# Splitting the convolution taps of two images between TensorE and VectorE, and when the gates of the second image stand in the queues

## The chip, the cores and the metric

The kernel runs on one core of a Trainium2 chip. The metric is the device time of one execution in microseconds (us). The kernel before took 3125.04 us, the median of three runs (3124.64 to 3130.11).

A core has five engines that run at the same time, each with its own queue of instructions in fixed order: TensorE (PE in the profile) multiplies matrices, VectorE (DVE) does elementwise work and reductions, ScalarE (ACT) functions such as Gelu, GpSimd (POOL) elementwise work and indirect DMAs, and SyncE (SP) issues plain DMAs. An instruction that waits holds back everything behind it in its queue.

## The reference

Two layers work on four images of 384 channels and 32×32 pixels. The first is an attention layer followed by a small MLP. The second, where the change is, adds a sum of depthwise convolutions and then a mixture of four experts:

```python
x = x + _L1_conv_ref(_ln_c(x), w77, b77, w53, ...)   # depthwise 7x7 + 5x3 + 3x5 + two separable ones
t = _to_tokens(x)
t = t + _L1_ffn_ref(_ln_t(t), gate_w, gate_b, w1, b1, w2, b2)

# in _L1_ffn_ref
probs = softmax(x @ gate_w + gate_b)                 # 4 experts, the two best of each token are kept
h = gelu(x @ w1[e] + b1[e])                          # 384 -> 1536
y = h @ w2[e] + b2[e]                                # 1536 -> 384
out = sum over e of masked[e] * y[e]
```

Everything is float32. All five convolutions fold into one 7×7 kernel per channel: 49 taps.

## The kernel before

The program has three parts. The first two, the projections and the attention (until about 1506 us of the span), are left as they are. The third, `rest_phase`, goes through the images b = 0 to 3.

**Per image.** `front(b)` loads the attention's output and x, projects (`project`: nine matmuls L977 for each half image, sums on VectorE L980), and runs the first layer's MLP (`net`: L999, L1012, Gelu L1022, L1016, L1029, the sum on VectorE L1030) for both halves. `banks` (L990) says how many accumulators the MLP's first matmuls rotate through: six for images 0 and 2, three for the others. `normalise` makes the normalised halves, and `image` (L1068) writes them into the single padded tile `img`, which holds one image at a time: the next image can be written only when the taps of the last have been read.

**Taps.** An image has 3 chunks of 128 channels by 32 rows, so 96 rows of a chunk. `convolve` (L1089) runs the taps on VectorE as one multiply-add each, all rows of a chunk at once (1024 elements per partition). Of image 0, `taps_by_matmul` gives 56 of the 96 rows to TensorE instead: chunk 2 whole in two parts of 16 rows (512 columns), and rows 8 to 32 of chunk 1 in two parts of 12 (384 columns). A part is 49 taps × 2 halves of matmuls with 64×64 diagonals of the tap's weights (L1133), two copies, two matmuls that fold the sums (L1144), and one addition on VectorE (L1147). The diagonals are made by GpSimd (L1115) and lie in the second pair of expert weight buffers, `wts[1]`, which is loaded by `preload` when image 0's taps are done.

**Gates and dispatch.** `gates(b)` multiplies the image by the gate weights (`gate_ps` L661, `logits_ps` L673), transposes it into token rows (`row_ps` L87, statistics on VectorE L89, a copy L92), picks two experts per token on VectorE and normalises the rows (L1191). `scatter(b)` ranks the tokens (`before_ps` L755, `count_ps` L757), and sends 16 indirect DMAs on GpSimd's queue (L1199) that write the rows into their experts' slots in DRAM; behind the first of them it works out which expert each block of the group has. `dispatch` is the two together.

**Blocks.** The experts run over blocks of 128 tokens of one expert, in four groups of 13, 16, 16 and 22; group b can begin when image b has been scattered. A block is 12 steps (`e_ps` L1294, Gelu L1297, `y_ps` L1272); its tokens come by an indirect DMA (L1243, transposed at L1256) that waits for the scatters of its group, its weights in two halves by indirect DMAs (L1262) into two pairs of buffers in turn, fetched three halves ahead; its end is the addition L1275.

**Order.** Image 0 is done ahead of the blocks (`first`), with image 1's front between its taps. Then image 0's dispatch is written, with the front of image 2 between its steps. The rest hangs on the blocks: `others` is a generator of side work (the taps of images 1, 2, 3, their dispatches, the front of image 3), and after each step of a block `more` adds 0.05 and 1.36 us to two clocks, of VectorE's and TensorE's work, and takes side steps, each with its two costs, while VectorE's clock is behind TensorE's:

```python
clock[0] += 0.05
clock[1] += 1.36
...
while clock[0] < clock[1] and spend(todo):
    pass
```

In `others`, the dispatch of image b is spent between the taps of image b + 1: step 2 and later of the taps takes the front of the next image (`side` or `later` by turns). A scheduler orders what is written; `pin` (`keep_in_program_order`) fixes an instruction's place on its engine, and `marks[b]` with `issue_after` holds the first additions of image b's taps behind a given instruction.

Of the kernel before, what the change touches and what calls it, by code (L numbers as in the profile page):

```python
# [13 lines left out]
ALU = mybir.AluOpType  # L14
# [8 lines left out]
KC = C // P  # L23
# [47 lines left out]
def bcast(ap, dim, n):  # L71

    dims = [list(d) for d in ap.ap]
    dims[dim] = [0, n]
    return bass.AP(ap.tensor, ap.offset, dims)
# [818 lines left out]
def rest_phase(tc, cst, x, ao_d, ins, xs_d, y_d, x2_d, out):  # L894
# [9 lines left out]
    with ExitStack() as es:  # L904
# [82 lines left out]

        def net(b, xs, rstd):

            banks = [(ps_h, "h", None)] * 3 + ([(ps_y, "y", 2)] * 2 + [(ps_y, "t", None)] if b in (0, 2) else [])  # L990
            if True:
                scale = to_partitions(nc, (small, ps_m, "m"), ident, one, rstd)
                scale_sb = work.tile([P, TOK], F32, tag="scale", name="scale")
                nc.scalar.copy(scale_sb, scale)


                ps = ps_m.tile([P, TOK], F32, tag="m", name="u_ps")
                for k in range(KC):
                    nc.tensor.matmul(ps, fold[:, k, :], xs[:, k, :], start=(k == 0), stop=(k == KC - 1))  # L999
                u = small.tile([P, TOK], F32, tag="u", name="u")  # L1000
                nc.vector.tensor_tensor(u, ps, scale_sb, ALU.mult)
                yield 1.4, 3.5

                po = ps_m.tile([P, TOK], F32, tag="m", name="o32_ps")
                pend = []
                for f0 in range(0, NF + 3, 3):
                    phs = []
                    for f in range(f0, min(f0 + 3, NF)):
                        pool, tag, bufs = banks[f % len(banks)]
                        ph = pool.tile([P, TOK], F32, tag=tag, name="f_ps", **({"bufs": bufs} if bufs else {}))  # L1010
                        lo = f % 4 * 32
                        nc.tensor.matmul(ph, c1t[lo : lo + 32, f // 4, :], u[lo : lo + 32, :], start=True, stop=True)  # L1012
                        phs.append((f, ph))
                    for f, hs in pend:
                        lo = f % 4 * 32
                        nc.tensor.matmul(  # L1016
                            po[lo : lo + 32, :], cp1t[:, f, :], hs, start=(f < 4), stop=(f >= NF - 4)
                        )
                    pend = []
                    for f, ph in phs:  # L1020
                        hs = hid.tile([P, TOK], F32, tag="hs", name="hs", bufs=HS)
                        nc.scalar.activation(hs, ph, AF.Gelu)  # L1022
                        pend.append((f, hs))
                    yield 0.0, 2.2
                o32 = small.tile([P, TOK], F32, tag="u", name="o32")
                nc.scalar.copy(o32, po)
                for m in range(KC):
                    ps = ps_h.tile([P, TOK], F32, tag="h", name="ffn_ps")
                    nc.tensor.matmul(ps, spread[:, m * P : (m + 1) * P], o32, start=True, stop=True)  # L1029
                    nc.vector.scalar_tensor_tensor(  # L1030
                        xs[:, m, :], ps, cp2[:, m : m + 1], xs[:, m, :], ALU.mult, ALU.add
                    )
                yield 2.1, 2.7
# [45 lines left out]
        def convolve(b, xb, parts):  # L1079


            with tc.issue_after(marks[b]) if b in marks else nullcontext():
                for k in range(KC):
                    nc.vector.tensor_scalar_add(xb[:, k, :], xb[:, k, :], cbias[:, k : k + 1])
            acc = xb.rearrange("p k (y x) -> p k y x", x=IMG)
            for dy in range(7):
                for dx in range(7):
                    for k, y0, y1 in parts:
                        nc.vector.scalar_tensor_tensor(  # L1089
                            acc[:, k, y0:y1], img[:, k, dy + y0 : dy + y1, dx : dx + IMG],  # L1090
                            w7[:, k, dy, dx : dx + 1], acc[:, k, y0:y1], ALU.mult, ALU.add,
                        )

                    if b:
                        tc.keep_in_program_order(nc.vector.memset(pause, 0.0))  # L1095
                    yield sum(0.12 + 0.0337 * (y1 - y0) for _, y0, y1 in parts) + 0.06, 0.0
            if b + 1 < B:
                nc.sync.dma_start(x2_d[:, b * N : (b + 1) * N].rearrange("(k p) n -> p k n", p=P), xb)
# [1 line left out]

        wts = [[wp.tile([P, WROW], F32, name=f"w{i}{fh}") for fh in range(2)] for i in range(2)]

        def preload(w, keep=lambda ins_: ins_):
            for fh in range(2):
                keep(nc.sync.dma_start(w[fh], ins["w12"][fh * P : (fh + 1) * P, :]))

        none = wp.tile([P, 2, 1], F32, name="none")
        nc.vector.memset(none, 0.0)
        def taps_by_matmul(xb, parts):

            def diagonals(k, w):
                d = w[:, : 49 * 64].rearrange("p (t m) -> p t m", m=64)
                nc.gpsimd.tensor_tensor(  # L1115
                    d, bcast(half.unsqueeze(1), 1, 49),
                    bcast(w7[:, k].rearrange("p y x -> p (y x)").unsqueeze(2), 2, 64), ALU.mult,
                )
                return d

            half = small.tile([P, 64], F32, tag="half", name="half", bufs=1)
            nc.vector.tensor_tensor(half, ident[:, :64], ident[:, 64:], ALU.add)
            diag = {k: diagonals(k, w) for k, w in zip(dict.fromkeys(k for k, *_ in parts), wts[1])}
            yield
            for k, y0, ny in parts:
                n = ny * IMG
                sums = [ps_y.tile([P, TOK], F32, tag="y", name="tap_ps", bufs=2) for _ in range(2)]
# [52 lines left out]
        def gates(b):  # L1180

            xb, im = xbs[b], images[b]
            rows = [new_row() for _ in range(nj)]
            logits = ps_m.tile([P, TOK], F32, tag="m", name="logits_ps")
            yield from gate_logits(nc, (ps_m, hid), ident, gw, xb, logits)
            mean, rstd = yield from token_stats(nc, stp, ident, xb, cst["eps5"], rows, 2)
            shift = small.tile([P, nj, 1], F32, tag="g_shift", name="g_shift")
            nc.vector.scalar_tensor_tensor(shift, mean, -1.0, rstd, ALU.mult, ALU.mult)
            yield from gate_weights(nc, small, logits, gb, rstd, im["mask"], im["top"])
            for j, row in enumerate(rows):  # L1190
                nc.scalar.activation(row, row, AF.Identity, bias=shift[:, j, :], scale=rstd[:, j, :])  # L1191
                im["rows"].append(row)
            yield 0.0, 0.0

        def new_row():
# [21 lines left out]
        def scatter(b, pause):  # L1217
# [3 lines left out]
            for j, rows in enumerate(im["rows"]):  # L1221
                for s in range(2):
                    write(rows, im["pos"][:, j, s : s + 1])
                if j == 0:
# [3 lines left out]
                    else:  # L1228
                        part = number_of_blocks(counts[b], False)
                        parts = [(done, part, b % 2 == 1)]  # L1230
                        parts.append((part, number_of_blocks(counts[b + 1], False), b % 2 == 0))
                        block_list(nc, small, pc, g, parts, None)
                    yield 4.0, 0.0
                yield pause, 0.0
            g["after"] = list(scattered)
# [146 lines left out]
        def first(halves, later):  # L1382


            half, own = IMG // 2, 8
            rest = (IMG - own) // 2
            taps = taps_by_matmul(
                xbs[0], [(2, 0, half), (2, half, half), (1, own, rest), (1, own + rest, rest)]
            )
            next(taps)  # L1390
            yield from image(halves)
            for i, _ in enumerate(convolve(0, xbs[0], [(0, 0, IMG), (1, 0, own)])):
                for _ in range(2 + (i % 4 == 3)):
                    next(taps, None)
                if i % 7 < 5:
                    next(later, None)
# [2 lines left out]
                        for _ in steps:  # L1399
                            pass  # L1400
                yield
            preload(wts[1])

        def others():

            later = iter(())
            for b in range(1, B):  # L1410
                if b > 1:
                    yield from image(halves[b])
                side, later = later, ahead(b + 1, halves[b + 1]) if b > 1 else iter(())
                for t, cost in enumerate(convolve(b, xbs[b], [(k, 0, IMG) for k in range(KC)])):
                    for start, steps in ((2, side), (12, later)):
                        more = next(steps, None) if t >= start else None
                        if more:
# [2 lines left out]
                yield from side  # L1420
                yield from later
                later = dispatch(b, 0.0 if b + 1 < B else 2.6)
            yield 6.0, 0.0
            yield from later

# [18 lines left out]
            pass  # L1444
        center(nc, ps_m, "m", one, gw)
        todo = others()
        for _ in first(halves[0], ahead(1, halves[1])):
            pass
        after_it = ahead(2, halves[2])
        for i, _ in enumerate(dispatch(0)):  # L1450
            if i == 0:
                result(image(halves[1]))
            if i == 10:
                marks[1] = latest(mybir.EngineType.DVE)
            for _ in range(3 if i > 5 else 0):
                next(after_it, None)
        result(after_it)
        clock = [0.0, 0.0]

        def spend(steps):  # L1460
            cost = next(steps, None)
# [125 lines left out]
```

## Time and profile before

The profile is of one execution on the chip, which took 3141.26 us itself, 16 us above the median of the three runs.

| | before |
|---|---|
| median of 3 runs | 3125.04 us (3124.64 to 3130.11) |
| the profiled execution | 3141.26 us |
| its span, first to last instruction | 3139.3 us |
| PE busy | 2942.2 us (94%) |
| DVE busy | 1935.2 us (62%) |
| ACT busy | 1370.1 us (44%) |
| POOL busy | 1168.1 us (37%) |
| granted TensorE clock, mean | 0.971 |

"Busy" is the time in which an engine executes something. In the view by slices, each digit is the busy share of one of 40 equal slices in tenths, and PEclk the clock that TensorE was granted. In a timeline line, the numbers are the start, the duration, the engine, the line of the program, the operation, what it writes and reads, the shapes and how many records, and in brackets the idle time before it and what ended it. One float32 matmul leaves two records. In the chain of waits, each line is a piece of work that ended last: start, duration, engine, what, line.

### The profile page before, as it was taken

How to read it: one execution, taken by the hardware profiler on the slowest of the kernel's cores; microseconds unless marked ns; L12 is line 12 of the kernel's file. 1: busy time of each engine (PE TensorE's matmuls, PEld its weight loads, DVE VectorE, ACT ScalarE, POOL GpSimd, SP SyncE). 2: the span in 40 equal slices, each digit the busy share in tenths (PEclk: the TensorE clock that was granted, in tenths of full speed). 3: DMA queues.
4: the chain of work that ended last, by engine and by line, in shares of the span. 5: the costliest groups of instructions: out<-in, count | busy, mean ns of one | idle time of the engine just before them, and what ended most of it. 6: DMA issues, size and time to landing. Idle time of an engine off the chain costs nothing.

```text
span 3139.3 us, 63791 instructions
## 1 busy us (share of the span) xinstructions
PE 2942.2 (94%) x25591; PEld 2026.2 (65%) x25591; DVE 1935.2 (62%) x3576; ACT 1370.1 (44%) x2833; POOL 1168.1 (37%) x1132
## 2 busy tenths in 40 slices
PE   8997999999999999999889999958999899999996
PEld 4544776777777777777433447734678677777775
DVE  2226777878787877787485699998999400001101
ACT  1115667666666666666202233323343423333332
POOL 2224747474746464646200222222143221124412
PEclk9998999999999999999989989988999999999998
DMA  3796566656565646563400305610444144375842
GB/s 128 261 316 204 130 197 136 202 134 202 133 204 130 209 125 209 125 210 97 162 19 33 136 23 222 257 56 26 169 177 172 41 174 182 138 277 210 301 178 73
DMA packets 262792, 500.56 MB, mean 159 GB/s; under 512 B 134736, under 2 KB 186832, under 8 KB 254816
## 3 DMA queue, kind: packets, MB, share of 16 engines
q1 hardware_dynamic: 169168, 247.12, 25.6%
q0 software_dynamic: 43424, 227.84, 19.7%
q10 hardware_dynamic: 49904, 21.53, 3.5%
q8 instruction: 201, 3.29, 0.4%
q14 instruction: 95, 0.78, 0.1%
HBM read 543.58 MB, written 152.37 MB: 222 GB/s over the span
## 4 chain that ended last, share of the span: by engine, by line
PE 73%; issue 9%; DVE 7%; POOL 4%; DMA 4%; ACT 2%; another core or an unknown queue 0%; SPq 0%; POOLq 0%; ACTq 0%; DVEq 0%
PE e_ps L1294 16%; PE y_ps L1272 15%; PE t_ps L410 7%; PE sc_ps L227 7%; PE av_ps L227 6%; PE tabq_ps L227 5%; DVE xb L1089 3%; PE a_ps L420 3%; PE tap_ps L1133 2%; DMA s<-sd 2%; PE tv_ps L227 2%; POOL bias L353 1%; PE proj_ps L977 1%; PE row_ps L87 1%; PE tabk_ps L227 1%
## 5 line engine op out<-in xcount | busy, mean ns | idle before, releaser
L1294 PEld LDWEIGHTS e_ps<-xT,w 128*128 128x128 f32 x4824 | 654.5, 192 | 214.1 <-issue 10.7
L353 POOL TENSOR_TENSOR bias<-b,s 128x416 f32<-128x416 f32 (+24 forms) x656 | 659.3, 1043 | 179.0 <-DMA s<-sd 165.1
L1294 PE MATMUL e_ps<-xT,w 128*128 128x128 f32 x4824 | 669.4, 276 | 8.6 <-DVE pause L1095 2.4
L1272 PE MATMUL y_ps<-w,eh 128*128 128x384 f32 x1608 | 651.9, 489 | 13.9 <-ACT eh L1297 11.9
L1089 DVE SCALAR_TENSOR_TENSOR xb<-img,pack,xb 128x1024 f32<-128x1024 f32 (+1 forms) x539 | 616.8, 1203 | 0.0
L1297 ACT ACTIVATE eh<-e_ps,w 128x128 f32<-128x128 f32 x804 | 293.2, 367 | 719.3 <-PE e_ps L1294 658.9
L1262 POOL DMA_INDIRECT w<-in_w,row x134 | 169.4, 1264 | 727.1 <-PE y_ps L1272 302.8
L402 DVE TENSOR_REDUCE extra<-arow 128x32 f32<-128x32 f32 (+24 forms) x768 | 381.3, 555 | 9.7 <-ACT arow L391 5.6
L381 DVE CUSTOM_DVE_ANT_0 arow<-sc_ps,bias 128x1024 f32<-128x1024 f32 x256 | 312.6, 1221 | 101.8 <-POOL bias L353 57.3
L410 PEld LDWEIGHTS t_ps<-ident,arow 128*128 128x128 f32 x2048 | 221.1, 142 | 175.2 <-ACT aT L411 100.6
L391 ACT ACTIVATE arow<-arow,nm 128x1024 f32<-128x1024 f32 x256 | 302.5, 1182 | 66.6 <-DVE nm L381 66.6
L1275 DVE TENSOR_TENSOR yo<-y_ps,w 128x384 f32<-128x384 f32 x67 | 37.1, 553 | 460.3 <-PE y_ps L1272 460.3
L411 ACT COPY aT<-t_ps 128x512 f32<-128x512 f32 x512 | 278.6, 603 | 95.2 <-PE t_ps L410 94.9
L410 PE MATMUL t_ps<-ident,arow 128*128 128x128 f32 x2048 | 283.1, 282 | 16.5 <-ACT arow L391 16.5
L227 PE MATMUL sc_ps<-kk,qs 48*32 48x512 f32 x4096 | 278.3, 606 | 8.7 <-DVE nm L381 8.1
L1272 PEld LDWEIGHTS y_ps<-w,eh 128*128 128x128 f32 x1608 | 246.7, 192 | 23.6 <-ACT eh L1297 13.8
L227 PEld LDWEIGHTS av_ps<-aT,vb 128*64 128x64 f32 x4096 | 222.3, 137 | 51.3 <-ACT aT L411 41.2
L227 PE MATMUL av_ps<-aT,vb 128*64 128x128 f32 x4096 | 237.7, 274 | 0.0
L318 DVE STREAM_TRANSPOSE b<-tabk_ps 128x480 f32<-128x480 f32 x256 | 218.4, 981 | 23.6 <-PE tabk_ps L227 22.2
L227 PE MATMUL tabk_ps<-tab,kq 48*128 48x480 f32 x512 | 223.2, 583 | 5.7 <-DVE b L318 5.7
L227 PE MATMUL tabq_ps<-tab,kq 48*128 48x480 f32 x512 | 220.3, 579 | 2.1 <-ACT aT L411 1.4
L1199 POOL DMA_INDIRECT xs_d<-rows,pos x64 | 78.5, 1227 | 337.7 <-DVE xb L980 253.0
(211 smaller groups left out, 3253.9 us busy)
## 6 DMA issues: line engine op xcount, KB each, us to landing
sd<-st SPq DMA_DIRECT2D x128, 480.0 KB
s<-sd SPq DMA_DIRECT2D x256, 240.0 KB
xs_d<-zero POOLq DMA_DIRECT2D x8, 3072.0 KB
tvw<-in_tv SPq DMA_DIRECT2D x120, 192.0 KB
y_d<-yo SPq DMA_DIRECT2D x67, 192.0 KB
qk_d<-qk_sb POOLq DMA_DIRECT2D x48, 256.0 KB
qs<-qk_d SPq DMA_DIRECT2D x256, 48.0 KB
kq<-qk_d ACTq DMA_DIRECT2D x56, 192.0 KB
```

Source lines behind the costliest of these rows:

```text
L227: ins = nc.tensor.matmul(*args, **kw)
L318: turn = nc.vector.transpose(b2.rearrange("p e y x -> p x (e y)")[:, i + j], ps[:, j, : SPAN * IMG])
L353: nc.gpsimd.tensor_tensor(bias[:, y0:y1, :], bass.AP(b2.tensor, b2.offset + (e * IMG + y0) * IMG, [list(b2.ap[0]), [(step * IMG + 1) * IMG ...
L381: nc.vector.tensor_tensor_reduce(s["flat"], ps.rearrange("p h n -> p (h n)"), s["bias"].rearrange("p y x -> p (y x)"), -SCALE, BIG, ALU.ad ...
L391: nc.scalar.activation(s["flat"], s["flat"], AF.Exp, bias=s["nm"], scale=-1.0, accum_out=dn[:, y % YT : y % YT + 1])
L402: pin(nc.vector.tensor_reduce(ex[:, i, :], a[:, p0:p1, :].rearrange("p y x -> p x y"), AX.X, ALU.add))
L410: pin(nc.tensor.transpose(pt[:, j, :], s["flat"][:, k0 : k0 + P], ident))
L411: pin(nc.scalar.copy(aT[:, 4 * g : 4 * g + 4, s["y"] % YB, :], pt))
L1089: nc.vector.scalar_tensor_tensor(acc[:, k, y0:y1], img[:, k, dy + y0 : dy + y1, dx : dx + IMG], w7[:, k, dy, dx : dx + 1], acc[:, k, y0:y1 ...
L1272: nc.tensor.matmul(py, hs, w[:, o : o + C], start=(ff == 0), stop=(ff == NF - 1))
L1294: nc.tensor.matmul(ph, w[:, o : o + P], xT[k][:, c, :], start=(c == 0), stop=(c == KC - 1))
L1297: nc.scalar.activation(hs, ph, AF.Gelu, bias=w[:, o : o + 1])
```

## The change

It has five parts.

1. Of image 0, TensorE does 40 of the 96 rows (chunk 2 whole, and rows 24 to 32 of chunk 1 in one part of 256 columns), VectorE chunk 0 and 24 rows of chunk 1. VectorE's taps of image 0 are pinned in program order, and the rhythm in which TensorE's taps are written between them changes.
2. The diagonals are made once, ahead of image 0's taps, and used again: TensorE does rows 0 to 16 of chunk 2 of image 1, written between the steps of image 0's dispatch, and VectorE the other 80 rows. The two buffers that hold the diagonals are loaded at two times: `wts[1][1]` after image 0's taps, `wts[1][0]` after those of image 1.
3. The dispatch of image 1 is started at once after the taps of image 1; after its first step, image 2 is written into `img`, and the dispatch is spent whole before image 2's taps. From image 2 on the order is as before. The mark that holds an image's first additions behind is set in `scatter`, behind the block list, for every image.
4. TensorE's clock starts at 25 instead of 0, so side work is taken earlier. In `gates`, steps are added after every second row for images 1 to 3.
5. The MLP of image 2 rotates through three accumulators instead of six.

```diff
-            banks = [(ps_h, "h", None)] * 3 + ([(ps_y, "y", 2)] * 2 + [(ps_y, "t", None)] if b in (0, 2) else [])
+            banks = [(ps_h, "h", None)] * 3 + ([(ps_y, "y", 2)] * 2 + [(ps_y, "t", None)] if b == 0 else [])
...
-                        nc.vector.scalar_tensor_tensor(
+                        ins_ = nc.vector.scalar_tensor_tensor(
                             acc[:, k, y0:y1], img[:, k, dy + y0 : dy + y1, dx : dx + IMG],
                             w7[:, k, dy, dx : dx + 1], acc[:, k, y0:y1], ALU.mult, ALU.add,
                         )
+                        if not b:
+                            pin(ins_)
...
-        def preload(w, keep=lambda ins_: ins_):
-            for fh in range(2):
+        def preload(w, keep=lambda ins_: ins_, which=range(2)):
+            for fh in which:
...
-        def taps_by_matmul(xb, parts):
-            def diagonals(k, w):
-                d = w[:, : 49 * 64].rearrange("p (t m) -> p t m", m=64)
+        def diagonals(chunks):
+            half = small.tile([P, 64], F32, tag="half", name="half", bufs=1)
+            nc.vector.tensor_tensor(half, ident[:, :64], ident[:, 64:], ALU.add)
+            diag = {}
+            for k, w in zip(chunks, wts[1]):
+                diag[k] = w[:, : 49 * 64].rearrange("p (t m) -> p t m", m=64)
                 nc.gpsimd.tensor_tensor(
-                    d, bcast(half.unsqueeze(1), 1, 49),
+                    diag[k], bcast(half.unsqueeze(1), 1, 49),
...
+        def taps_by_matmul(xb, made, parts):
+            half, diag = made
...
                 im["rows"].append(row)
+                if b and j % 2:
+                    yield 0.0, 0.0
...
                         block_list(nc, small, pc, g, parts, None)
+                    marks[b + 1] = latest(mybir.EngineType.DVE)
...
-            half, own = IMG // 2, 8
-            rest = (IMG - own) // 2
-            taps = taps_by_matmul(
-                xbs[0], [(2, 0, half), (2, half, half), (1, own, rest), (1, own + rest, rest)]
-            )
-            next(taps)
+            half, own = IMG // 2, 24
+            taps = taps_by_matmul(xbs[0], made, [(2, 0, half), (2, half, half), (1, own, IMG - own)])
             yield from image(halves)
             for i, _ in enumerate(convolve(0, xbs[0], [(0, 0, IMG), (1, 0, own)])):
-                for _ in range(2 + (i % 4 == 3)):
+                for _ in range(1 + i % 4 // 2 + (i % 7 == 0)):
                     next(taps, None)
...
-            preload(wts[1])
+            preload(wts[1], which=(1,))
...
-            later = iter(())
+            half, later = IMG // 2, iter(())
             for b in range(1, B):
-                if b > 1:
+                if b > 2:
                     yield from image(halves[b])
                 side, later = later, ahead(b + 1, halves[b + 1]) if b > 1 else iter(())
-                for t, cost in enumerate(convolve(b, xbs[b], [(k, 0, IMG) for k in range(KC)])):
+                parts = [(k, 0, IMG) for k in range(KC - 1)] + [(KC - 1, half if b == 1 else 0, IMG)]
+                for t, cost in enumerate(convolve(b, xbs[b], parts)):
...
                 later = dispatch(b, 0.0 if b + 1 < B else 2.6)
+                if b == 1:
+                    yield next(later)
+                    yield from image(halves[2])
+                    yield from later
...
         todo = others()
+        made = diagonals((2, 1))
         for _ in first(halves[0], ahead(1, halves[1])):
             pass
-        after_it = ahead(2, halves[2])
+        taps, later = taps_by_matmul(xbs[1], made, [(2, 0, IMG // 2)]), ahead(2, halves[2])
         for i, _ in enumerate(dispatch(0)):
             if i == 0:
                 result(image(halves[1]))
-            if i == 10:
-                marks[1] = latest(mybir.EngineType.DVE)
-            for _ in range(3 if i > 5 else 0):
-                next(after_it, None)
-        result(after_it)
-        clock = [0.0, 0.0]
+            for steps in (taps, taps, taps, later, later, later) if i > 5 else ():
+                next(steps, None)
+        for steps in (taps, later):
+            result(steps)
+        preload(wts[1], which=(0,))
+        clock = [0.0, 25.0]
```

## The prediction

> **What bounds the kernel now.** I read the page's 40 slices first, each 78.5 us long.
>
> ```profile
> PE   8997999999999999999889999958999899999996
> DVE  2226777878787877787485699998999400001101
> PEclk9998999999999999999989989988999999999998
> ```
>
> TensorE (PE) is full from slice 21 on, but for one hole (5 and 8, from about 2041 us), where VectorE (DVE) stays at 9. The change touches only this part. So I cut it by the events of its code into windows: start and end, us, busy time by engine, granted TensorE clock, DMA share, GB/s.
>
> ```profile
> 1592.80:1764.50 171.70, 152.05 (x972) 56.48 (x964) 110.36 (x162) 24.13 (x44) 0.00 (x0) 0.91 0.07 26
> 1764.50:1796.30 31.80, 26.83 (x95) 13.74 (x95) 24.23 (x123) 13.05 (x23) 8.96 (x9) 0.89 0.76 270
> 1796.30:1849.30 53.00, 46.03 (x174) 16.46 (x173) 50.60 (x75) 20.36 (x35) 21.35 (x17) 0.84 0.15 50
> 1849.30:2068.00 218.70, 217.87 (x1326) 170.27 (x1325) 217.61 (x263) 69.70 (x180) 41.30 (x30) 1.00 0.45 174
> 2068.00:2128.60 60.60, 16.73 (x46) 8.15 (x44) 56.41 (x150) 10.52 (x16) 24.12 (x20) 0.67 0.24 85
> 2128.60:2200.00 71.40, 67.71 (x330) 36.37 (x331) 63.13 (x79) 28.82 (x57) 11.37 (x9) 0.95 0.05 15
> ```
>
> Row 1 is image 0's taps, bound by TensorE (152 of 172). Row 2 is image 0's gates up to image 1's first tap, row 3 ends at the first expert matmul. Row 4, the 13 blocks of group 0, has TensorE and VectorE both full. Row 5 is the hole: TensorE works 16.7 of 60.6 us. The timeline and the chain of waits say for what (time, duration, engine):
>
> ```profile
> 2046.02 2.77 PE L661 MATMUL gate_ps<-xb,pack 128*32 128x512 f32 x12
> 2128.61 0.90 PE L1256 MATMUL xT_ps<-ident,xg 128*128 128x128 f32 x3 [28.71 <-DMA xg<-xs_d,slot]
> 2131.53 4.92 PE L977 MATMUL proj_ps<-at,pack 128*128 128x512 f32 x6
> ```
> ```profile
> 2069.69 2.37 DVE xb L1089 x2
> 2073.43 4.30 ACT rows L1191 x7
> 2089.56 1.19 DVE xb L1089
> 2097.92 1.09 POOL xs_d L1199
> 2116.70 2.02 POOL xs_d L1199
> 2125.47 3.10 DMA xg<-xs_d,slot
> ```
>
> Gates of image 1 start in group 0's last block, at 2046. Their small VectorE steps stand between image 2's taps of 1.19 us, 16 scatters follow, and group 1's tokens arrive 82.6 us after the gate matmul.
>
> The groups of window 1 (busy us, mean ns of one, idle before) price the taps:
>
> ```profile
> L1089 DVE SCALAR_TENSOR_TENSOR xb<-img,pack,xb 128x1024 f32<-128x1024 f32 x49 | 62.6, 1278 | 0.0
> L1133 PE MATMUL tap_ps<-img,w 64*64 64x512 f32 x348 | 48.5, 624 | 0.0
> L1133 PE MATMUL tap_ps<-img,w 64*64 64x384 f32 x392 | 39.0, 495 | 0.0
> L1089 DVE SCALAR_TENSOR_TENSOR xb<-img,pack,xb 128x256 f32<-128x256 f32 x49 | 23.4, 477 | 0.0
> ```
>
> **What the Trainium skill says.** "TensorE: Matmul & The Clock Gate", section "What's actually happening": the array drops to half clock after an idle window and needs some 3.4 us of work to return. The trace agrees: after 28.7 us idle six projection records take 4.92 us (2.84 at 1603.9, with the clock up) and the clock reads 0.67. "SBUF — State Buffer", section "🔬 SBUF: two separate sides": VectorE with two SBUF inputs and GpSimd exclude each other. A scatter's issue takes 2.02 us where it meets taps, 0.97 otherwise.
>
> **The change, part by part.** Sums are against the profiled execution (3141.26 us, its span 3139.3, 16 us above the median).
>
> *Image 0's taps (1592.8 on).* Back to back, VectorE's 1024-element tap takes 1.205 us (three in 3.67) and the pair with 256 elements 1.595 (16 pairs in 25.55). That gives about 0.39 for 256, and at the same slope 0.935 for 768 and 0.66 for 512. VectorE: 49 × (1.205 + 0.935) = 105 instead of 78, +26.7. TensorE's 512-column record takes 0.115 us (116 in 13.32), the 384-column one 0.086; a part has 196 records. Before 2 × 22.5 + 2 × 16.9 = 78.8; after 2 × 22.5 + about 11.5 = 56.5, −22.3. TensorE could then end at 1592.8 + 152 − 22 ≈ 1723, VectorE at 1592.8 + 105 taps + 32 other work (110.4 − 78.2) + 8 waits ≈ 1737. VectorE takes over: gate matmul at 1737 for 1764.5, −28.
>
> *Image 0's gates.* 36 tap matmuls (72 records × 0.115 = 8.3) and four row transposes, which wait for image 2's projection sums on VectorE, now stand before the rank matmul (`before_ps`). So 31.8 becomes about 42, and image 1's first VectorE tap comes at 1779 instead of 1796.3.
>
> *First tap to first expert.* TensorE has the rest of 22.5 us of image 1's taps here, in a window with only 7 us idle; VectorE's order has 49 tap operations before image 2's last residual sum (L1030), where 30 stood: 19 × 1.1 = 21, and 1.4 for the sum of TensorE's part. 53 becomes 76; first expert matmul at 1855, **+5.5** (bounds −6 to +15: TensorE waiting less, or the two engines waiting on each other).
>
> The diagonals are made earlier on an idle POOL (0.00 in row 1): nothing. The reload of the second weight buffer waits for image 1's taps, behind image 2's loads on SP's queue. It is 2.5 MB, 9 us at the 270 GB/s of row 2, needed a block (16.1 us) after the first expert; if the cover goes, up to 9 us.
>
> *Gates of image 1.* They move in TensorE's order from block 11.9 to block 8. A steady block takes 16.11 us, so that is about 1855 + 130 = 1985. Image 1's VectorE taps took 203.6 us and lose 26.7: done at 1779 + 177 = 1956, 29 us ahead. If late, all expert work stands behind this matmul. With no taps between, its list is ready by some 2035; group 0 ends about 2083. The hole goes: 60.6 − 16.7 = **−44**, and the cold clock (0.95 over 71.4 us) **−4**.
>
> *Price of gates at once.* Group 0's 218.7 us less 13 × 16.11 leaves 9.3 for gates spread over a block. Image 3's gates, concentrated, made their block 39.5 us, 23.4 extra. I take 19: **+10** (0 to +14). Gates of image 3 have yields between rows: **−3** (0 to −6).
>
> *POOL.* Image 1's 16 scatters stand between the two weight fetches of block 10: 16 × 1.3 to 2 = 21 to 32 us of POOL, with fetches issued 1.5 blocks (24 us) ahead: **+3** (0 to +8).
>
> *Side work 25 us earlier, three banks for image 2's net, image 2's taps behind the gates.* VectorE idles from 1956 to 1985, so image 2's taps start at about 2012, as before (2004.5), while TensorE reaches image 2's gates some 30 us sooner: their slack falls from about 40 to 12, that of image 3's is about as thin. **+5** (0 to +25).
>
> Sum: 5.5 − 44 − 4 + 10 − 3 + 3 + 5 = −27.5. On the median, 3125 − 28 = **3097 us**.
>
> **Rivals.**
> *More gain* (0.15): gates at once cost no more than spread ones, nothing late at image 2's gates, first expert no later: −44 − 4 − 3 = −51, 3074. For: the concentrated cost of image 3's gates held four table loads of 1.28 us. Against: VectorE's longer list before the first expert.
> *Less gain* (0.22): the first expert +12, gates at once +14, scatters +6, the gates of image 2 and 3 late by 5 together: −48 + 37 = −11, 3114. For: every one of these is inside its bounds, and TensorE's order has no room to pass a late VectorE.
> *Within 0.2%* (0.07): the hole moves whole to image 2's gates, where conv 2 (233 us from 2004.5) would have to end over 50 us later than now.
> *Slower* (0.14): with image 0's taps pinned, image 1's front (its sums L980, L1001, L1030, each waiting for TensorE) stands at fixed places between them, so a late TensorE stops VectorE and the taps behind. A net's chain (its Gelus 13.0 us, its matmuls 9.3 and 8.5 in window 1, for two nets) is 15 us; if VectorE waits out both, 30 us, the first stage keeps its old length, and a like wait after the first tap of image 1 puts the first expert late. It decides from a first expert at 1885, 36 us late: gates of image 1 then hold TensorE as well, and the time is 3125 − 28 + 36 to 45, about 3137. For: window 1 had 17.4 us of TensorE idle waiting for such a sum. Against: TensorE loses 22 us there and runs ahead.
> That the gates do not move is excluded by the order of TensorE's queue, which the program fixes.
>
> **How the numbers follow.** The forecast (0.42): 3085 to 3108, from the bounds of its terms taken two at a time. With the chances above, the range 3066 to 3125 leaves out the slower case, half of the even one and the edge of the best. About 0.2% (6.3 us) is what a measurement can tell from no change: faster 0.79, same 0.07, slower 0.14.
>
> **What would show it.** Image 0's gate matmul near 1737 (1764 would refute the first step), first expert at 1850 to 1865; image 1's gates between blocks 8 and 9 with VectorE idle up to 30 us before them; no TensorE gap between groups 0 and 1, and the projections there at 2.8 us for six records; a block of some 35 us at block 8. I am wrong if a TensorE gap over 10 us waits for VectorE at the gates of image 1, 2 or 3, or a weight fetch at block 10 is late by more.

## The result

The change made the kernel faster: 3101.35 us median (3099.03 to 3105.85, four runs) against 3126.77 us (3124.64 to 3130.11, four runs) on the same chip. The ratio is 0.9919, with a 95% interval of 0.9902 to 0.9937. The forecast was 3097, in a range of 3066 to 3125.

The page of the changed kernel by slices; the hole (the digits 5 and 8 of TensorE before) is gone:

```profile
PE   8997999999999999999899789989999999999996
DVE  2226777878787877787578899589999610001101
PEclk9998999999999999999999889999999999999998
```

The same stretch in windows cut at the same events (start and end, us, busy time and records by engine, granted TensorE clock, DMA share, GB/s):

```profile
1592.00:1738.10 146.10, 123.47 (x772) 45.81 (x764) 132.14 (x159) 23.07 (x42) 0.00 (x0) 0.91 0.06 24
1738.10:1777.60 39.50, 39.46 (x186) 16.17 (x187) 26.28 (x121) 13.05 (x23) 3.33 (x3) 0.93 0.44 150
1777.60:1854.50 76.90, 66.88 (x282) 23.65 (x281) 74.18 (x89) 21.84 (x37) 38.66 (x23) 0.84 0.23 81
1854.50:2096.50 242.00, 226.69 (x1342) 175.87 (x1340) 192.31 (x357) 80.98 (x197) 69.95 (x51) 0.97 0.47 179
2096.50:2224.80 128.30, 121.81 (x620) 75.05 (x621) 127.26 (x174) 47.91 (x97) 18.95 (x13) 1.00 0.21 74
```

The first stage (row 1) is now VectorE's, 132 of 146 us. Row 3 is 24 us longer than before, group 0 (row 4) 23 us longer, and row 5, blocks 13 to 16, runs without a hole. TensorE's timeline at the two group boundaries of interest:

```profile
1987.91 2.77 PE L661 MATMUL gate_ps<-xb,pack 128*32 128x512 f32 x12
2049.73 1.65 PE L1301 MATMUL e_ps<-xT,w 128*128 128x128 f32 x6 [11.45 <-DMA w<-in_w,row]
2090.63 2.74 PE L977 MATMUL proj_ps<-at,pack 128*128 128x512 f32 x6
2095.81 0.49 PE L1263 MATMUL xT_ps<-ident,xg 128*128 128x128 f32 x3
```

The gates of image 1 stand at 1988, the first tokens of group 1 are transposed at 2095.81 without a wait, and six projection records cost 2.74 us where they cost 4.92 after the hole. New is a wait of 11.45 us for a weight half. TensorE's longest waits from 1590 to 2600 us (total, times, longest):

```profile
PE gate_ps L661 <- DVE xb L1089: 11.5, 1, 11.5
PE e_ps L1301 <- DMA w<-in_w,row: 11.4, 1, 11.4
PE y_ps L1279 <- ACT eh L1304: 8.2, 7, 2.6
```

The first is image 0's gate matmul, which waits for VectorE's last tap. Where the time went, in the profiled executions (before 3141.26, after 3105.85 us):

| stretch | before | after | difference |
|---|---|---|---|
| first tap of image 0 to first expert matmul | 256.5 | 262.5 | +6.0 |
| group 0, to the end of its 13th block | 218.7 | 242.0 | +23.3 |
| the next four blocks, with the hole | 182.7 | 128.4 | −54.3 |
| the next 13 blocks | 217.8 | 221.2 | +3.4 |
| two blocks with the gates of image 3 | 53.7 | 50.5 | −3.2 |

That is −24.8, and −25.6 with the 0.8 us by which the taps start sooner. The medians differ by 25.4, which is close, though both executions lie above their medians (by 14.5 and 4.5 us). The profiled executions are further apart, 35.4 us, because that of before lost another 9 us after these stretches, 8 of them in its last group, where the two kernels do the same. Two of its blocks near 2850 took 19.1 and 18.9 us, for example, where every later profile has 16.1 and 17.4.

### The profile page after: what moved, and what is told of

Same layout as the page of the kernel before. It is cut to its first block, busy times and chain, and to the rows that moved or that the text cites. A ratio compares the mean times of both kernels' runs of the same rounds, so it can differ in the third digit from the quotient of the medians.

```text
span 3104.1 us, 63791 instructions
## 1 busy us (share of the span) xinstructions
PE 2943.5 (95%) x25591; PEld 2026.7 (65%) x25591; DVE 1936.6 (62%) x3576; ACT 1375.3 (44%) x2835; POOL 1188.2 (38%) x1132
## 4 chain that ended last, share of the span: by engine, by line
PE 76%; DVE 9%; issue 6%; DMA 4%; POOL 3%; ACT 2%; SPq 0%; POOLq 0%; ACTq 0%; DVEq 0%
PE e_ps L1301 16%; PE y_ps L1279 16%; PE t_ps L410 7%; PE sc_ps L227 7%; PE av_ps L227 7%; PE tabq_ps L227 5%; DVE xb L1089 4%; PE a_ps L420 3%; PE qk_ps L175 2%; PE tap_ps L1137 2%; PE proj_ps L977 2%; DMA s<-sd 2%; PE tv_ps L227 2%; POOL bias L353 1%; PE tabk_ps L227 1%
## 5 line engine op out<-in xcount | busy, mean ns | idle before, releaser
L1301 PEld LDWEIGHTS e_ps<-xT,w 128*128 128x128 f32 x4824 | 655.4, 192 | 224.6 <-DMA w<-in_w,row 12.1
L1301 PE MATMUL e_ps<-xT,w 128*128 128x128 f32 x4824 | 670.4, 276 | 20.0 <-DMA w<-in_w,row 11.4
L1089 DVE SCALAR_TENSOR_TENSOR xb<-img,pack,xb 128x1024 f32<-128x1024 f32 (+2 forms) x539 | 616.6, 1203 | 0.0
L1205 POOL DMA_INDIRECT xs_d<-rows,pos x64 | 92.3, 1442 | 263.6 <-DVE b_prod L860 239.5
```

What stands on the lines that cost most here:

```text
L1089: ins_ = nc.vector.scalar_tensor_tensor(acc[:, k, y0:y1], img[:, k, dy + y0 : dy + y1, dx : dx + IMG], w7[:, k, dy, dx : dx + 1], acc[:, k ...
L1301: nc.tensor.matmul(ph, w[:, o : o + P], xT[k][:, c, :], start=(c == 0), stop=(c == KC - 1))
```

## The experiments

All times are medians of four or more runs. They come in three sets, e1 to e4, e5 to e8 and e9 to e12, and the kernel before took 3126.2, 3126.8 and 3123.6 us beside them. A difference between two sets is therefore uncertain by some 3 us; the ratios are each to the kernel before in the same set.

| run | edit | median | ratio to before, 95% |
|---|---|---|---|
| the change | all | 3101.4 | 0.9902 to 0.9937 |
| e1 | before + order of image 1's gates | 3112.1 | 0.9950 to 0.9972 |
| e6 | e1 + mark | 3098.4 | 0.9897 to 0.9944 |
| e5 | before + pin | 3111.0 | 0.9933 to 0.9966 |
| e7 | change − pin | 3117.4 | 0.9966 to 0.9983 |
| e2 | change − order | 3085.3 | 0.9856 to 0.9888 |
| e3 | change − split | 3080.9 | 0.9834 to 0.9867 |
| e8 | change − split − order | 3107.5 | 0.9924 to 0.9960 |
| e9 | e3 + six accumulators | 3071.6 | 0.9815 to 0.9848 |
| e11 | e9 with the clock at 0 | 3082.9 | 0.9852 to 0.9885 |
| e4 | change + scatters spread | 3090.0 | 0.9875 to 0.9911 |
| e10 | e9 + scatters spread | 3062.3 | 0.9783 to 0.9815 |
| e12 | change − gate steps | 3098.1 | 0.9894 to 0.9927 |

My theory was the forecast's: the split shortens the first stage and buys early gates, and the gates in one run remove the hole. The rivals: the split carries the gain by itself, or the order does, or neither and the pin and the clock do it. The split, the clock and the mark were not run alone on the kernel before, and three smaller parts of the change were not isolated: the mark of image 1, the rhythm of TensorE's taps and the second time at which the weight buffers are loaded.

### The order of the gates, alone

e1 puts this into the kernel before:

```diff
-                if b > 1:
+                if b > 2:
                     yield from image(halves[b])
...
                 later = dispatch(b, 0.0 if b + 1 < B else 2.6)
+                if b == 1:
+                    yield next(later)
+                    yield from image(halves[2])
+                    yield from later
```

> The kernel before with one part of the change alone: image 1's dispatch straight after its taps, image 2 and its taps behind it; taps split, clock and accumulators as before. In TensorE's order the gates of image 1 come at block 11.25 instead of 11.9. Theory A (what pays is that the gates of image 1 are no longer cut up by image 2's taps, so the tokens come sooner after the gate matmul; the split of the taps only buys margin): first expert at 1849 as before, gate matmul near 2031, tokens ready near 2085, a hole of 15 to 20 us left of the 44 at the end of group 0, gain 20 to 30 us, about 3100 to 3107 against 3127. Rival B (the gain comes from the taps split, which lets the gates stand at block 8; without it they come too late): hole of 35 us or more, gain under 10, 3117 or more. Rival C (what limits is how late VectorE is with all taps, so that the hole goes over to image 2's gates): a wait of TensorE over 15 us at the gate matmul of image 2.

It gave 3112.1, between Theory A and Rival B, and the hole stayed. TensorE in e1, then VectorE in e1 ahead of it:

```profile
2110.65 0.90 PE L1256 MATMUL xT_ps<-ident,xg 128*128 128x128 f32 x3 [34.57 <-DMA xg<-xs_d,slot]
```
```profile
2000.65 2.07 DVE L1084 TENSOR_SCALAR xb<-xb,pack 128x1024 f32<-128x1024 f32 x3
2002.63 4.88 DVE L1089 SCALAR_TENSOR_TENSOR xb<-img,pack,xb 128x1024 f32<-128x1024 f32 x4
...
2038.54 1.03 DVE L89 BATCH_NORM_STATS2 s_st<-row_ps 128x6 f32<-128x384 f32 x2
2039.57 1.25 DVE L1089 SCALAR_TENSOR_TENSOR xb<-img,pack,xb 128x1024 f32<-128x1024 f32 x1
```

Image 2's taps were written behind the gates, and yet stand ahead of and between their steps (2002.6 for gates at 2033.1): the scheduler may move what is not held. So the mark is a part of the order, which e1 left out. e6 adds it:

```diff
                         block_list(nc, small, pc, g, parts, None)
+                    if b:
+                        marks[b + 1] = latest(mybir.EngineType.DVE)
```

> The kernel before with the order of image 1's dispatch and with the mark too, which holds the first additions of image 2's taps behind image 1's block list, so that VectorE's taps can't slip ahead of the gates as they did without it (first tap of image 2 at 2002.6, gates at 2033). Theory A (what cost the 77 us from gate matmul to tokens there was taps slipping between the gate steps): tokens 50 to 55 us after the gate matmul, hole 10 to 15 us instead of 34.6, 3090 to 3098. Rival B (at block 11.25 the gates are simply too late, whatever stands between): hole above 25 us, 3105 to 3112. Rival C: image 2's taps now end too late for its own gates, and TensorE waits there by 10 us or more.

The line of e6 that answers to e1's:

```profile
2083.56 0.90 PE L1258 MATMUL xT_ps<-ident,xg 128*128 128x128 f32 x3 [12.56 <-DMA xg<-xs_d,slot]
```

The tokens come 55 us after the gate matmul (2028.2) instead of 77, the wait is 12.6 us, as Theory A has it, and the time 3098.4: order and mark alone bring as much as the whole change. The time is 0.4 us above the range that I gave. No wait showed at image 2's gates.

### The pin, alone and undone

```diff
-                        nc.vector.scalar_tensor_tensor(
+                        ins_ = nc.vector.scalar_tensor_tensor(
...
+                        if not b:
+                            pin(ins_)
```

> The kernel before with only image 0's VectorE taps pinned in program order. In VectorE's order the projection sums of image 1 (L980) then stand behind tap 16, 18, 20, 24, 30 and 32 instead of 32, 39, 45, 53, 69 and 77. Theory A (the forecast's first step was right in size but not in cause: the pin, not the split, shortens the first stage): image 0's gate matmul 152 us after the first tap instead of 172, first expert 6 to 8 us sooner, the hole before group 1 as long as before; 3117 to 3121 against 3126. Rival B (the split shortens the stage): gate matmul at 170 to 173 us after the first tap, no gain.

The waits of TensorE in the first stage, in the kernel before and in e5, and e5's window:

```profile
PE row_ps L87 <- DVE xb L980: 17.4, 4, 6.3
```
```profile
PE all_ps L117 <- DVE s_dg L115: 3.1, 2, 2.2
PE gate_ps L661 <- DVE xb L1089: 2.2, 1, 2.2
```
```profile
1591.75:1742.90 151.15, 143.76 (x974) 53.66 (x967) 108.42 (x160) 24.18 (x44) 0.00 (x0) 1.00 0.08 30
1782.30:1825.50 43.20, 35.10 (x151) 12.42 (x152) 43.20 (x60) 19.01 (x33) 28.54 (x20) 0.96 0.23 74
```

With the split as before, the pin takes the first stage from 171.7 to 151.2 us, and the change only from there to 146.1. In those 20.5 us, 8.3 are busy time of almost the same matmuls (152.05 us for 972 records at a clock of 0.91, 143.76 for 974 at 1.00), the rest waits that are gone. The gain was larger than expected, 15.8 us, and the first expert came 22.7 us sooner after the first tap, not 6 to 8: row 3 was shorter too. Undoing the pin in the changed kernel:

> The changed kernel without the pin on image 0's taps; all else as changed. The sums of image 1's front stand 1 to 11 taps later among VectorE's taps, those of its second net behind the last tap. Theory A: the first stage grows by 8 to 20 us from 146, the first expert moves by about as much, 3107 to 3120 against 3101 for the change. Rival B (with less work TensorE has slack of 11 us at the end of the stage, which hides the later sums): within 3 us of the change.

3117.4, 16 us slower, within Theory A. Left free, VectorE's queue puts a sum that TensorE needs (L1001) behind 13 taps (14.03 us), and TensorE waits in e7:

```profile
1692.59 14.03 DVE L1089 SCALAR_TENSOR_TENSOR xb<-img,pack,xb 128x1024 f32<-128x1024 f32 x13
1706.53 0.68 DVE L1001 TENSOR_TENSOR u<-u_ps,scale 128x512 f32<-128x512 f32 x1
```
```profile
1707.27 2.08 PE L1012 MATMUL f_ps<-u,pack 32*128 32x512 f32 x6 [20.52 <-DVE u L1001]
```

### The order, undone in the changed kernel

```diff
                 later = dispatch(b, 0.0 if b + 1 < B else 2.6)
-                if b == 1:
-                    yield next(later)
-                    yield from image(halves[2])
-                    yield from later
```

with image 2 written as before (`b > 1`). The mark of image 2 then has no effect, as before the change: its taps are begun before `scatter` sets it. The same holds for e8 below.

> The changed kernel with only the order undone: image 2's taps run on while image 1's gates are spent between them, as before; taps split, clock at 25 and the rest stay. The gates of image 1 stand from block 8.7 to 11.8 in TensorE's order. Theory A as first put (the gates must stand in one run): the steps between taps make the tokens about 30 us later after the gate matmul, ready near 2090, hole up to 15 us, gain 10 to 20, 3107 to 3117. Rival B (early gates are enough, by the split and the clock): no hole at the end of group 0, no block of 30 us at the gates, no late weight fetch, 3088 to 3098, as good as the whole change or better.

Rival B: 3085.3 us, 16 us faster than the change. The gates are cut up as before and take some 100 us from gate matmul to tokens, but they start at block 8.7 and so end near the end of group 0. First transpose of group 1 in e2:

```profile
2098.30 0.80 PE L1263 MATMUL xT_ps<-ident,xg 128*128 128x128 f32 x3 [2.53 <-DMA xg<-xs_d,slot]
```

Group 0 took 224.1 us, not 242.0: neither a block of 30.5 us with all gates, nor a late weight half. That the gates must stand in one run has fallen, for gates this early.

### The split, undone

```diff
-            half, own = IMG // 2, 24
-            taps = taps_by_matmul(xbs[0], made, [(2, 0, half), (2, half, half), (1, own, IMG - own)])
+            half, own = IMG // 2, 8
+            rest = (IMG - own) // 2
+            taps = taps_by_matmul(xbs[0], made, [(2, 0, half), (2, half, half), (1, own, rest), (1, own + rest, rest)])
...
-                for _ in range(1 + i % 4 // 2 + (i % 7 == 0)):
+                for _ in range(2 + (i % 4 == 3)):
...
-                parts = [(k, 0, IMG) for k in range(KC - 1)] + [(KC - 1, half if b == 1 else 0, IMG)]
+                parts = [(k, 0, IMG) for k in range(KC - 1)] + [(KC - 1, 0, IMG)]
...
-        taps, later = taps_by_matmul(xbs[1], made, [(2, 0, IMG // 2)]), ahead(2, halves[2])
+        taps, later = iter(()), ahead(2, halves[2])
```

> The changed kernel with the taps split as before: TensorE 56 rows of image 0 and none of image 1; order of the gates, clock, accumulators and yields stay. The gates of image 1 stand at block 9.7. Theory A: the first stage is 26 us longer and the next two shorter, first expert at 1849, so 5 us before that of the changed kernel; image 1's VectorE taps end near 2000, just ahead of the gates at about 2005; no hole; 3090 to 3100. Rival B (the split carries the gain): TensorE waits for VectorE at image 1's gates by 10 us or more or the hole comes back by 15 or more; 3108 to 3120.

3080.9: beside the new order, the split costs 20.5 us. The first stage is 152.3 us, not 26 longer as I had written but 6, since the pin does the work there. The first expert comes 249.9 us after the first tap instead of 262.5, and the weight half is late by 3.90 instead of 11.45 us; these 12.6 + 7.5 = 20.1 us are about the difference. No hole came back. With the order undone too:

> The changed kernel with both the taps split and the order of image 1's gates undone; pin, clock at 25, yields, accumulators stay. Gates of image 1 at block 10.3 to 13 of TensorE's order. Theory A (order and split are two ways to the same end, tokens before the end of group 0, and one of them is needed): gate matmul near 2005, tokens 80 us later, hole 20 to 30 us, 3095 to 3108. Rival B (the clock and the pin alone do it): hole below 8 us, 3080 to 3088.

3107.5, at the upper end of Theory A. TensorE between the end of group 0 and group 1's first transpose in e8:

```profile
2058.45:2103.50 45.05, 20.59 (x53) 9.61 (x52) 45.02 (x116) 0.30 (x1) 25.34 (x20) 0.74 0.22 79
```

It is idle for 24.5 of 45.1 us, so the hole has come back in part, and the tokens come 95.6 us after the gate matmul (2007.9). Here, with the gates at block 10.3, the order is worth 26.6 us (e3 against e8). The split is worth 22.2 where the order is undone (e2 against e8), and costs 20.5 where it is not. Order and split are two ways to the same end, and the change pays for both.

### The accumulators

The split forces three accumulators on image 2's MLP, since TensorE's part of image 1's taps sits in the other three. e9 is e3 with six again:

```diff
-            banks = [(ps_h, "h", None)] * 3 + ([(ps_y, "y", 2)] * 2 + [(ps_y, "t", None)] if b == 0 else [])
+            banks = [(ps_h, "h", None)] * 3 + ([(ps_y, "y", 2)] * 2 + [(ps_y, "t", None)] if b in (0, 2) else [])
```

> The changed kernel with the old split of the taps, and with image 2's MLP on six accumulators again, as before; TensorE's part of image 1's taps took three of them. Against the old split with three accumulators (3081) this is one change of size. Theory A (three accumulators make image 2's two MLPs, which stand in front of the first expert, 6 to 8 us longer each, because a first matmul must wait for a Gelu): first expert 12 to 15 us sooner after the first tap (235 to 238 us, not 250), and 3066 to 3074, less than 15 because VectorE is not sooner done with image 1 (10 us ahead of its gates there). Rival B (the accumulators don't matter, that front hides behind VectorE's taps): first expert at 248 or later, 3078 to 3084.

3071.6, and the first expert at 237.0: Theory A. First tap of image 1 to first expert in e3 and in e9:

```profile
1781.60:1837.50 55.90, 50.87 (x151) 17.77 (x152) 46.00 (x62) 19.86 (x33) 25.67 (x20) 0.70 0.17 57
```
```profile
1779.60:1824.60 45.00, 39.07 (x151) 13.30 (x152) 43.53 (x61) 19.28 (x33) 28.04 (x20) 0.85 0.21 71
```

151 records take 50.87 us with three accumulators and 39.07 with six, at clocks of 0.70 and 0.85. TensorE is idle for 5.0 and 5.9 us of the two windows, so nearly all of the difference shows as longer matmuls and not as waits (more in the last section). The other runs with the old split and the pin agree: 57.9 us with three accumulators (e8), 43.2 to 44.2 with six (e5, e10, e11). By the medians six accumulators bring 9.2 us, by the ratios to the kernel before 6.5. Six accumulators together with the new split weren't tried, for the reason given.

### The clock, the scatters, the gate steps

e11 is e9 with `clock = [0.0, 0.0]`.

> The kernel with old split and six accumulators, and TensorE's clock starting at 0 instead of 25: side work 1.6 blocks later in TensorE's order, gates of image 1 at block 11.25. Theory A (the tokens of group 1 must come before group 0 ends, 50 us after the gate matmul): they come 10 us too late, a hole of 8 to 15 us, 5 to 12 us over the run with the clock at 25. Rival B (with gates in one run the start of the clock no longer matters): within 3 us.

3082.9, +11.3, Theory A, with a wait a little over the 8 to 15 us expected; the first transpose of group 1 in e11:

```profile
2068.92 0.90 PE L1263 MATMUL xT_ps<-ident,xg 128*128 128x128 f32 x3 [15.58 <-DMA xg<-xs_d,slot]
```

e4 spreads the scatters of image 1 in the changed kernel:

```diff
-                later = dispatch(b, 0.0 if b + 1 < B else 2.6)
+                later = dispatch(b, {1: 2.0, 2: 0.0, 3: 2.6}[b])
```

> The changed kernel with image 1's 16 scatters written over about a block (two units of VectorE's cost after each row) instead of in one piece, so that a weight fetch stands between them on GpSimd's queue; the later side work moves about one block back. If the 11.4 us that TensorE waits for a weight half in block 10 come from the 16 scatters ahead of its fetch: that wait falls under 3 us, and the time by 6 to 11 us against the changed kernel, to 3090 to 3095. If the wait is the transfer's own (three fetches at once): it stays near 11 and the time near 3101.

3090.0, −11.4: the wait for the weight half is gone, block 10 takes 16.1 us instead of 28.2. TensorE's longest wait from 1990 to 2110 us in e4, and its wait for a weight half there in e3 and e9:

```profile
PE y_ps L1279 <- ACT eh L1304: 2.8, 3, 1.6
```
```profile
PE e_ps L1301 <- DMA w<-in_w,row: 3.9, 1, 3.9
```
```profile
PE e_ps L1301 <- DMA w<-in_w,row: 1.9, 1, 1.9
```

In the changed kernel GpSimd's queue shows why it came (timeline, with the first and last of the 16 scatters):

```profile
2010.17 1.03 POOL L1205 DMA_INDIRECT xs_d<-rows,pos  x1 [0.85 <-ACT eh L1304]
...
2037.53 0.97 POOL L1205 DMA_INDIRECT xs_d<-rows,pos  x1 [0.30 <-issue]
2038.80 2.09 POOL L1269 DMA_INDIRECT w<-in_w,row  x1 [0.30 <-DVE xb L1089]
```

and the chain of waits what followed:

```profile
2037.51 1.28 DVE xb L1089
2038.80 10.89 DMA w<-in_w,row
2049.73 1.65 PE e_ps L1301 x6
```

The fetch was issued 28.6 us after the first scatter and then took 10.9 to land. The same on e9 gave the fastest kernel:

> The same with image 1's scatters spread over a block too. Theory A: a weight half is late by 3.9 us with the old split, so at most 4 us are to be had here, and the side work moved by one block costs nothing: 3 to 4 us under the run with six accumulators. Rival B: the 11 us that spreading brought the changed kernel came mostly from elsewhere than the late fetch, so it brings 8 or more here too, or it loses because the tokens of group 1 come later.

3062.3, 61 us (2.0%) under the kernel before in its set, and 9.4 under e9, which is Rival B's figure. The two profiles differ by 3 us only, as Theory A says, with a wait of 1.94 us for the fetch in e9. The profiled execution of e9 was 5 us faster than its other runs, so the wait may vary; what the other 6 us are is open. e12 is the changed kernel without the added `yield` in `gates`:

> The changed kernel without the added steps after every second row of the gates; the gates of images 2 and 3 then stand in fewer places of TensorE's order. Theory A, the forecast's term: 0 to 6 us slower than the change, 3101 to 3107. Rival B: no difference that is measured, because the eight row copies are ScalarE's and its queue catches up.

3098.1, with an interval that overlaps the change's (each is 25.4 us under the kernel before in its own set): Rival B's outcome, no difference that can be told. Its reason wasn't tested.

## Why the prediction was right, and which of its steps were not

Image 0's gate matmul: 1738.1 for 1737. TensorE would have been ready at 1726.6 (1738.1 − 11.5) for 1723. First tap of image 1: 1777.6 for 1779. First expert: 1854.5 for 1855. Image 1 done on VectorE: 1955.5 for 1956. Its gates: 1987.9 for 1985. Image 2's first tap: 2013.8 for 2012. These places were worked out within 4 us. The end of group 0 was not: 2096.5 for about 2083. Causes and prices were less sure, and that the sum came within 5 us is partly luck: group 0 grew by 23.3 us where +13 was forecast, and the next four blocks lost 54.3 where −48 was. One of the prediction's own signs of being wrong came too, a weight fetch at block 10 late by more than 10 us (11.45).

- *"VectorE takes over: gate matmul at 1737 ..., −28."* The size was right, the cause not. I gave the gain to the split and named the pin only as a risk, in the slower rival. e5 and e3 show the reverse: with the old split and the pin the stage is 151 to 152 us, and the split takes off another 5 to 6. Without the pin the split takes off 9.5 (162.2 us in e7). The 17.4 us that TensorE waited for projection sums were in the profile, and VectorE's new order had those sums earlier; I didn't join the two.
- *"53 becomes 76."* Measured 76.9. The split's part, 21 + 1.4, is borne out by e3 (76.9 − 55.9 = 21.0). That it fits is luck, for two terms that I left out of it cancelled (the three banks are named only under the later +5): three accumulators, +11 (e3 against e9), and the pin, −8 to −10 (45.0 in e9, 43.2 in e5, against 53.0).
- *"The hole goes: −44, and the cold clock −4."* Measured −54.3 over the next four blocks. The hole is right: TensorE's idle time there fell from 50.8 to 6.5 us, −44.3. The slow clock was mis-sized: before, this stretch had 131.88 us of busy TensorE for 644 records, after 121.81 for 620, at clocks of 0.87 and 1.00.
- *"Price of gates at once: +10."* Their block takes 30.5 us, 14.4 over a steady one, where the spread gates of before cost 3.6 over the group's last five blocks (84.1 − 5 × 16.11), with their rest in the hole: +10.8. The sum was right, its two terms, 19 and 9.3, were not: of the 9.3 that I put down to the gates, 5.8 are group 0's first block (21.9 us), which is as long in the changed kernel (21.4).
- *"POOL: +3 (0 to +8)."* Mis-sized, and outside its bounds: the late half cost 12.1 us. I set 21 to 32 us of scatters against 24 us of lead, and left out that the transfer, 10.9 us, must fit into the lead as well. e4 gives it back.
- *"Their slack falls ...: +5."* No wait at the gates of image 2 or 3, and +3.4 us in those blocks, no cause shown.
- *"Gates of image 3: −3."* Measured −3.2 in the profile; e12, with 50.4 us for these two blocks against 50.5, shows that the added steps are not what it comes from.

Of the rivals, "less gain" had the mechanism that came (a late weight half), the slower one did not come: in the first stage VectorE waited for TensorE by 13.2 us in all, where I had put 8, and by 3.9 at most at one sum (two waits for L1030, 5.3 together).

By parts, where a run isolates one: order with mark −28 (e6), pin −16 (e5, e7), clock −11 (e11 against e9), split +20 (e3), accumulators +6.5 to +9 (e9 against e3), steps 0. They sum to between −28 and −26 for a change of −25.4, but that is no check. Each was measured on another base, and they don't add: the order, −28 on the kernel before, costs 16 in the changed kernel (e2), and the split, +20 there, is worth 22 without the order.

## What to carry to other kernels

Before a gain is credited to a new division of work, run the ordering part of the edit by itself: here the order with its mark alone brought as much as the whole change, and the pin alone 16 us, while moving the taps lost 20 us beside the new order and gained 22 without it. A dispatch that must precede the next group has to be early enough, and how early depends on whether it is in one piece: in one piece, gates at block 9.7 left no wait (e3, e9) and gates at 11.25 a wait of 15.6 us (e11); cut up, gates at 8.7 left 2.5 us (e2) and gates at 10.3 TensorE idle for 24.5 (e8). When many small DMAs go into a queue ahead of a fetch, set their time plus the fetch's own against its lead.

## What the runs showed of the hardware

The granted clock fell to half without a long wait. In the first of image 2's two MLPs, six output records took 1.93 us in e3, about twice what they took in e5 (1.06), the same shapes:

```profile
1783.41 3.05 PE L1012 MATMUL f_ps<-u,pack 32*128 32x512 f32 x6 [0.67 <-ACT hs L1022]
1786.39 1.93 PE L1016 MATMUL o_ps<-hs,pack 128*32 128x512 f32 x6
1788.24 2.87 PE L1012 MATMUL f_ps<-u,pack 32*128 32x512 f32 x6
```
```profile
1787.15 1.06 PE L1016 MATMUL o_ps<-hs,pack 128*32 128x512 f32 x6
1788.13 1.13 PE L1012 MATMUL f_ps<-u,pack 32*128 32x512 f32 x6
```

The first lines are e3, with three accumulators, where a first matmul waits for a Gelu; the second e5, with six. The windows of these MLPs in e3 and e5, and one of the second MLP in e9:

```profile
1786.00:1798.00 12.00, 12.00 (x34) 2.94 (x34) 11.81 (x13) 4.25 (x9) 9.87 (x8) 0.50 0.28 100
```
```profile
1786.00:1795.00 9.00, 9.00 (x38) 2.76 (x38) 9.00 (x12) 4.85 (x10) 7.48 (x6) 1.00 0.25 93
```
```profile
1802.00:1814.00 12.00, 12.00 (x38) 2.33 (x36) 12.00 (x14) 5.53 (x11) 7.05 (x5) 0.50 0.13 33
```

From 1765 to 1800 us the longest TensorE wait is 1.5 us in both e3 and e5, and e3 has one more, the 0.67 us. "TensorE: Matmul & The Clock Gate", section "What's actually happening", in the Trainium skill says that the clock follows how busy the array has been lately, in windows of about 3.4 us. That fits, but its table puts the half clock after an idle window of that length, and in e3 no wait was half as long. The price is in the matmuls: TensorE's busy time from image 1's first tap to the first expert is 50.87 us in e3, 39.07 in e9 and 35.10 in e5. Three accumulators are not the only way there. With six, e9's second MLP ran at 0.50 for 12 us after a wait of 4.12 us, while e5's, after one of 4.14, was back at 1.00 by 1807, some 5 us later. Why these two differ isn't shown.

A scatter's issue on GpSimd took between 0.97 and 4.01 us in the changed kernel:

```profile
2014.28 4.01 POOL L1205 DMA_INDIRECT xs_d<-rows,pos  x1 [0.30 <-issue]
2021.46 0.97 POOL L1205 DMA_INDIRECT xs_d<-rows,pos  x1 [0.30 <-issue]
2022.73 2.02 POOL L1205 DMA_INDIRECT xs_d<-rows,pos  x1 [0.30 <-issue]
```
```profile
2021.43 4.88 DVE L1089 SCALAR_TENSOR_TENSOR xb<-img,pack,xb 128x1024 f32<-128x1024 f32 x4
2025.05 0.06 DVE L1097 MEMSET pause<- 128x1 f32 x1
```

All three lie beside VectorE's taps, the 0.97 too, so "where it meets taps" in the prediction isn't the whole condition. Issues that began with one of the small memsets between taps (2025.06, for example) took 0.97, those that began beside a tap mostly 2.02. What decides isn't shown.
